# Second modulation and weight preparation on GpSimd, shared rotary keys projected ahead of the latent norm, three Newton steps

## The chip, the core and the metric

The kernel runs on one core of a Trainium2 chip. A core has five engines with a queue each: TensorE (PE in the profile; PEld is its loading of weights), VectorE (DVE), ScalarE (ACT), GpSimd (POOL) and SyncE (SP), which here only issues DMA transfers. An engine works through its queue in order; semaphores make it wait for others. The metric is the device time of one execution in microseconds, lower is better.

## The reference, cut to what matters

Two layers with adaptive layer norm over x of shape (8, 512, 128), that is 8 batches of 512 positions with 128 channels, everything in float32.

```python
def layer(x, c, wmod, attn, ffn):
    mod = (silu(c) @ wmod).reshape(8, 6, 1, -1)
    sa, ca, ga, sb, cb, gb = (mod[:, j] for j in range(6))
    ga = (2 * (ga >= 0) - 1) * maximum(abs(ga), 0.25)
    gb = (2 * (gb >= 0) - 1) * maximum(abs(gb), 0.25)
    x = x + ga * attn(layernorm(x) * (1 + ca) + sa)
    return x + gb * ffn(layernorm(x) * (1 + cb) + sb)
```

- Layer 0's attention is an RWKV time mix: each of the three projections of a mix of x and x shifted by one position, a recurrence over time with running maximum, then a projection. Its feed-forward is a linear layer with both operands quantized to a 6-bit grid in blocks of 32.
- Layer 1's attention has 16 heads of 32 plain and 64 rotary dimensions. A latent `x @ [w_cq, w_ckv]` is normed by its root mean square, 96 columns for the queries and 32 for keys and values. Three branches share the queries: causal attention on keys from the latent, with one rotary key `rope(x @ w_krope) / 16` shared by all heads; attention on the 32 positions of the highest score; and causal attention on keys straight from x. A softmax gate weighs the three.
- Layer 1's feed-forward is a gated recurrence over the 8 batches, each batch one step, whose final state enters every output.

## The kernel before, in words

**Layout.** Activations are held channels by positions, 128 x 512 a batch, or as four tiles of 128 positions by 128 channels for norms. Weights come in four packs (`pa` with layer 0's and the modulations, `pb` with layer 1's attention and a few of layer 0's, `pt` with the rotary tables, `pc` with the recurrence).

**Before the loop.** Up to the `manual_schedule` block the framework's scheduler orders every engine's queue: of the instructions that it takes to be ready, the one written first goes first. The source writes `modulate(0)`, the mixing weights, then the first `FIRST` = 14 steps of layer 0 for batch 0, then `remaining()`: the second modulation, the quantized weight of layer 0's linear layer, the scaling of the attention's weights by the norm's gains (L269 to L273), the halving of the recurrence's weights (L276), and the causal mask. After it the rest of layer 0 for batch 0, the preparation of batch 0, the first group's queries and keys, and the shared rotary keys follow, since the loop needs them.

**The loop.** Inside the block the order of PE, DVE, ACT and POOL is the order of the source. There are 192 units: 8 batches, 4 groups of 4 heads, 2 causal branches, and 3 parts of the triangle of positions. For each unit PE computes scores (`score`, L793), DVE adds the mask and reduces the rows (`lowered`, L805), ACT takes exponentials and sums (`raised`, L814), POOL divides (`normalised`, L823), PE transposes the result (`weigh`, L837; ACT copies it, L603), and PE multiplies with the values (`values`, L851). A unit's scores are written two units ahead of its transposition.

**Chains beside the loop.** Three generators run beside it: `layer0()` (mix and linear layer of each batch), `before()` (`prepare(b)`: norm, latent, shared keys, gate, the chosen 32 positions) and `recurrence()`. `advance` moves each by one step, four times a unit. A `yield 0` or `yield TR` goes on at the next advance, a smaller number waits for that many advances first, and `yield M` (M = 100) goes on only where `advance` is called with M, at the last of a unit's four. `need(name, b)` advances all chains until a step has been reached: `made` (the transposed latent nqT is there), `shared` (the rotary keys k1R are), `gate`, `chosen`.

**What the change touches.**
- `rsqrt` (L89 to L97): a first guess by integer arithmetic (L91) and four Newton steps of three DVE instructions each (L94, L95, L96), with a `yield 0` after each step. It is called in each layer norm (`ln_norm`: mix, linear, prepare, and two of the recurrence) and in the latent's norm.
- `modulate(l)` (L216 to L237): tanh on ACT, two DVE instructions, six matmuls, a copy out of PSUM (L228), and the rest on 128x8 pieces (L230 to L237), all on DVE.
- `prepare(b)` (L430 on): norm, transposition to hT (L442), the latent (L449, L451), its squares on POOL (L456), their sums (L460, L461), `rsqrt`, the scaling (L465 on DVE for the queries' 96 columns, L468 on POOL for the others), transposition (tpq) and copy to nqT (L475), a DMA of its last 32 rows to `latent` (L478), `made`; then `shared_keys`, `shared`; then the gate.
- `shared_keys(b)` calls `rotary`: two projections of hT (L638, named k1Rm), each multiplied twice by the tables on DVE (L619, L620, L624, L626), and a subtraction and an addition on POOL (L625, L627).
- The recurrence of a batch of layer 0 (L332 to L383): three scans on DVE, exponentials on ACT, a product (L364) and a sum (L372) on POOL, a division (L381, L383); then the output matmul (L386).

Of the kernel before, what the change touches and what calls it, by code (L numbers as in the profile page):

```python
# [14 lines left out]
ALU = mybir.AluOpType  # L15
# [3 lines left out]
B, T, D = 8, 512, 128  # L19
# [39 lines left out]
def adaln_kernel(ctx: ExitStack, tc: tile.TileContext, x, pa, pb, pc, pt, out):  # L59
# [29 lines left out]
    def rsqrt(dst, v, n, key):  # L89

        V.tensor_scalar(dst.bitcast(U32), v.bitcast(U32), -0.5, float(0x5F3759DF), ALU.mult, ALU.add)  # L91
        t = small.tile([128, n], FP, name=f"rt_{key}", tag=f"rt{n}")
        for _ in range(4):
            V.scalar_tensor_tensor(t, dst, -0.5, dst, ALU.mult, ALU.mult)  # L94
            V.tensor_tensor(t, t, v, ALU.mult)  # L95
            V.scalar_tensor_tensor(dst, t, 1.5, dst, ALU.add, ALU.mult)  # L96
            yield 0  # L97
# [117 lines left out]

    def modulate(l):  # L216
        c_in = WA[f"cT{l}"]

        sg = part(B)
        S.activation(sg, c_in, AF.Tanh, scale=0.5)  # L220
        si = sil0 if l == 0 else part(B)
        V.tensor_scalar(sg, sg, 0.5, 0.5, ALU.mult, ALU.add)
        V.tensor_tensor(si, sg, c_in, ALU.mult)
        ps = bank([128, 6, B], f"modps{l}")
        for j in range(6):
            PE.matmul(ps[:, j, :], lhsT=WA[f"wmod{l}"][:, j * 128 : (j + 1) * 128], rhs=si, start=True, stop=True)
        m = mods[l]
        V.tensor_copy(m, ps)  # L228
        for j in (1, 4):
            V.tensor_scalar(m[:, j, :], m[:, j, :], 1.0, None, ALU.add)  # L230
        for j in (2, 5):
            sgn = part(B)
            V.tensor_scalar(sgn, m[:, j, :], 0.0, 2.0, ALU.is_ge, ALU.mult)
            mag = part(B)
            V.scalar_tensor_tensor(mag, m[:, j, :], -1.0, m[:, j, :], ALU.mult, ALU.max)
            V.tensor_scalar(mag, mag, 0.25, None, ALU.max)
            V.scalar_tensor_tensor(m[:, j, :], sgn, -1.0, mag, ALU.add, ALU.mult)  # L237

    modulate(0)

# [10 lines left out]
    def remaining():  # L251

        modulate(1)


        wq = part(128, 4, 32)
        for _ in mx_quantize(
            wq, WA["fw"].rearrange("p (n k) -> p n k", k=32), 4,
            lambda n: part(128, 4, 32), "w",
        ):  # L260
            pass
        wps = bank([128, 128], "wps")
        PE.transpose(wps, wq.rearrange("p n k -> p (n k)"), ident)
        S.copy(wqT, wps)
        V.tensor_scalar(gbias, mod0[:, 5, :], WA["fbias"], None, ALU.mult)

        qscale = 1.0 / math.sqrt(HD)
        gq = part(1, rows=QL)
        V.tensor_scalar(gq, WB["g"][0:QL, :], qscale, None, ALU.mult)  # L269
        V.tensor_scalar(wd[0:QL, :], wd[0:QL, :], gq, None, ALU.mult)  # L270
        V.tensor_scalar(wd[QL:128, 0:512], wd[QL:128, 0:512], WB["g"][QL:128, :], None, ALU.mult)
        V.tensor_scalar(WB["wdk"][0:KVL, :], WB["wdk"][0:KVL, :], WB["g4"][0:KVL, :], None, ALU.mult)
        V.tensor_scalar(WB["wkr"], WB["wkr"], 1.0 / H, None, ALU.mult)  # L273

        for n in ("ufT", "uiT", "ucT", "uoT", "bf", "bi"):
            V.tensor_scalar(WC[n], WC[n], 0.5, None, ALU.mult)  # L276
# [153 lines left out]
    def prepare(b):  # L430
# [8 lines left out]
        transposed(tp, xn)  # L439
        hT = keep.tile([128, T], FP, name=f"hT1_{b}", tag="hT")  # L440
        hsum = small.tile([128, 1], FP, name=f"hsum_{b}", tag="hsum")
        S.activation(hT, tp, AF.Identity, bias=sa[:, b : b + 1], scale=ca[:, b : b + 1])  # L442
# [9 lines left out]
        sq = work("p2", [128, NC, 128], f"sq_{b}")  # L452
        yield 0
        hbc = pw.tile([128, 128], FP, name=f"hbc_{b}", tag="hbc")
        G.tensor_copy(hbc, hsum.to_broadcast([128, 128]))
        G.tensor_tensor(sq, cq, cq, ALU.mult)  # L456
        yield 1
        ss = small.tile([128, 2, NC], FP, name=f"ss_{b}", tag="ss")
        for i, (cols, n) in enumerate(((slice(0, QL), QL), (slice(QL, 128), KVL))):
            V.tensor_reduce(ss[:, i, :], sq[:, :, cols], AX.X, ALU.add)  # L460
            V.tensor_scalar(ss[:, i, :], ss[:, i, :], 1.0 / n, RMS_EPS, ALU.mult, ALU.add)  # L461
            yield 0
        rr = small.tile([128, 2, NC], FP, name=f"rr_{b}", tag="rr")
        yield from rsqrt(rr.rearrange("p k c -> p (k c)"), ss.rearrange("p k c -> p (k c)"), 2 * NC, f"rms{b}")
        V.tensor_tensor(  # L465
# [254 lines left out]
    def shared_keys(b):  # L720

        hT, nqT, _, _ = made_of[b]
        for i, _ in enumerate(rotary(pb_, "k1R", f"{b}", hT, WB["wkr"], (pw, ("p2", "p3")))):
# [147 lines left out]

    made_of, latent_of, k1_of, chosen_of, q_of, k3_of, v_of, sel_of, out_of, acc_of, pT_of, rot_of, xnf_of, h2_of = ({} for _ in range(14))

# [276 lines left out]
```

## Time and profile before

| | |
|---|---|
| time, median of 3 runs | 1703.07 us (1700.11 to 1705.38) |
| the profiled execution's span | 1703.6 us, 39936 instructions |
| granted TensorE clock, mean | 0.960 |
| first instruction of the loop's scores (L793) | 98.95 us |
| last projection of the attention (L862) | 1671.8 us |
| POOL's four forms of L823 | 426, 516, 620, 775 ns for 128, 256, 384, 512 columns |
| DVE multiplication 128x512 by a table (L624) | 676 ns |

How to read the profile's rows. A row of the time line has start and duration in us, engine, line, operation, what is written <- what is read, shape, and in brackets how long the engine was idle before it and whom it waited for. A row of the chain of waits has start, duration, engine, tile and line: it is followed back from the last instruction, each time to what released it. A row of the table by stage has the stretch, its length, the busy time (and count of instructions) of PE, PEld, DVE, ACT and POOL, the granted clock of TensorE as a fraction, the DMA share and GB/s. Matmul ends are modelled, so a busy PE is not a PE at its peak.

### The profile page before, as it was taken

How to read it: one execution, taken by the hardware profiler on the slowest of the kernel's cores; microseconds unless marked ns; L12 is line 12 of the kernel's file. 1: busy time of each engine (PE TensorE's matmuls, PEld its weight loads, DVE VectorE, ACT ScalarE, POOL GpSimd, SP SyncE). 2: the span in 40 equal slices, each digit the busy share in tenths (PEclk: the TensorE clock that was granted, in tenths of full speed). 3: DMA queues.
4: the chain of work that ended last, by engine and by line, in shares of the span. 5: the costliest groups of instructions: out<-in, count | busy, mean ns of one | idle time of the engine just before them, and what ended most of it. 6: DMA issues, size and time to landing. Idle time of an engine off the chain costs nothing.

```text
span 1703.6 us, 39936 instructions
## 1 busy us (share of the span) xinstructions
PE 1571.0 (92%) x14773; PEld 936.0 (55%) x14773; DVE 1267.4 (74%) x4262; ACT 1154.0 (68%) x3248; POOL 936.7 (55%) x1370
## 2 busy tenths in 40 slices
PE   3487999899999999999899999989999999999997
PEld 2244655555555655565456555655555665656663
DVE  6669868875789859876879769867789677756543
ACT  2144777665776867777666677766776777777883
POOL 2155567554666557564556457564566556655651
PEclk8578999998999999999999999999999999999999
DMA  4000000000000000000000000000000100000002
GB/s 170 0 3 1 2 1 4 7 2 13 3 2 8 8 8 4 1 8 14 3 2 2 8 8 3 2 2 20 3 2 14 32 14 3 2 14 14 1 11 66
DMA packets 13778, 20.55 MB, mean 12 GB/s; under 512 B 912, under 2 KB 9104, under 8 KB 13456
## 3 DMA queue, kind: packets, MB, share of 16 engines
q1 hardware_dynamic: 13584, 17.99, 3.1%
q8 instruction: 118, 1.93, 0.5%
q14 instruction: 76, 0.62, 0.1%
HBM read 11.70 MB, written 5.77 MB: 10 GB/s over the span
## 4 chain that ended last, share of the span: by engine, by line
PE 63%; DVE 26%; ACT 5%; issue 3%; POOL 3%; DMA 0%; POOLq 0%; SPq 0%; ACTq 0%; DVEq 0%
PE s L793 19%; PE t L837 12%; DVE p L805 7%; PE o L851 7%; PE s L755 2%; PE k3Rm L638 2%; PE qRm L638 2%; ACT p L814 2%; PE k3Np L610 1%; PE v1p L651 1%; PE op L862 1%; PE o L738 1%; PE qNp L610 1%; PE k0Np L610 1%; ACT pT L603 1%
## 5 line engine op out<-in xcount | busy, mean ns | idle before, releaser
L823 POOL TENSOR_SCALAR p<-p,rs 128x512 f32<-128x512 f32 (+3 forms) x1024 | 578.2, 584 | 389.3 <-DVE rs L819 219.1
L805 DVE CUSTOM_DVE_ANT_0 p<-s,mask 128x512 f32<-128x512 f32 (+3 forms) x1024 | 442.4, 477 | 177.5 <-PE s L793 175.5
L814 ACT ACTIVATE p<-p,nm 128x512 f32<-128x512 f32 (+3 forms) x1024 | 560.0, 553 | 14.1 <-DVE nm L805 13.9
L603 ACT COPY pT<-t 128x384 f32<-128x384 f32 (+1 forms) x768 | 354.6, 521 | 183.9 <-PE t L837 181.3
L837 PE MATMUL t<-ident,p 128*128 128x128 f32 x2560 | 367.2, 281 | 34.7 <-ACT pT L603 7.2
L837 PEld LDWEIGHTS t<-ident,p 128*128 128x128 f32 x2560 | 276.0, 142 | 160.1 <-issue 114.6
L814 ACT ACTIVATION_READ_ACCUMULATOR p<-p,nm 128x1 f32 x1024 | 196.8, 192 | 0.0
L793 PE MATMUL s<-k3R,qR 32*128 32x128 f32 (+3 forms) x2048 | 185.7, 453 | 4.4 <-DVE nm L805 3.2
L793 PE MATMUL s<-k1R,qR 32*128 32x512 f32 (+3 forms) x2048 | 186.2, 453 | 2.1 <-POOL k1R L625 2.1
L851 PE MATMUL o<-pT,v 128*32 128x512 f32 (+3 forms) x2048 | 153.2, 440 | 0.0
L793 PEld LDWEIGHTS s<-k3R,qR 32*128 32x128 f32 x2048 | 97.5, 186 | 83.4 <-DVE nm L805 30.8
L793 PEld LDWEIGHTS s<-k1R,qR 32*128 32x128 f32 x2048 | 105.7, 187 | 48.8 <-issue 15.2
L851 PEld LDWEIGHTS o<-pT,v 128*32 128x32 f32 x2048 | 60.4, 110 | 111.1 <-issue 100.3
L793 PE MATMUL s<-k0N,qN 32*128 32x512 f32 (+3 forms) x1024 | 102.4, 435 | 0.0
L793 PE MATMUL s<-k3N,qN 32*128 32x512 f32 (+3 forms) x1024 | 95.9, 431 | 0.0
L625 POOL TENSOR_TENSOR k3R<-k3R,rt_k3R 128x512 f32<-128x512 f32 x32 | 40.7, 1273 | 84.5 <-DVE rt_k3R L624 84.5
L805 DVE DVE_READ_ACCUMULATOR2_ANT nm<- 128x1 f32 x1024 | 82.4, 80 | 0.1
L765 POOL TENSOR_TENSOR p<-p,m 128x512 f32<-128x512 f32 x32 | 33.5, 1048 | 67.6 <-DVE m L764 67.6
L793 PEld LDWEIGHTS s<-k0N,qN 32*128 32x128 f32 x1024 | 60.4, 188 | 17.0 <-issue 2.5
L638 PE MATMUL qRm<-nqT,wb 96*128 96x512 f32 x128 | 68.6, 619 | 1.2 <-ACT nqT L475 0.7
L603 ACT COPY accT<-o 128x512 f32<-128x512 f32 x32 | 18.8, 586 | 71.1 <-PE o L851 71.1
L793 PEld LDWEIGHTS s<-k3N,qN 32*128 32x128 f32 x1024 | 54.4, 187 | 21.9 <-issue 14.9
(315 smaller groups left out, 2450.3 us busy)
## 6 DMA issues: line engine op xcount, KB each, us to landing
wb<-pb_dram SPq DMA_DIRECT2D x1, 3731.0 KB, 14.3
x<-x_dram SPq DMA_DIRECT2D x8, 256.0 KB, 4.1
x1all<-x SPq DMA_DIRECT2D x7, 256.0 KB, 2.0
h2all<-h SPq DMA_DIRECT2D x7, 256.0 KB, 2.0
h2o<-h2all SPq DMA_DIRECT2D x7, 256.0 KB, 2.6
x_first<-x1all SPq DMA_DIRECT2D x4, 256.0 KB, 3.4
out_dram<-x_first SPq DMA_DIRECT2D x4, 256.0 KB, 2.2
out_dram<-x SPq DMA_DIRECT2D x4, 256.0 KB, 2.3
```

The costliest lines, as they stand in the source:

```text
L603: S.copy(dst, src)
L610: PE.matmul(ps, lhsT=w[:, g * 128 : (g + 1) * 128], rhs=src, start=True, stop=True)
L625: G.tensor_tensor(lo, lo, r[0], ALU.subtract)
L638: PE.matmul(ps, lhsT=w[:, i * 128 : (i + 1) * 128], rhs=src, start=True, stop=True)
L755: PE.matmul(sp[h][to, :], lhsT=k[js, g, :], rhs=q[js, h * half : (h + 1) * half], start=(i == 0), stop=(i == 2), skip_group_check=True,)
L765: G.tensor_tensor(p2, p2, m2.unsqueeze(2).to_broadcast([128, T // 32, KEEP]), ALU.subtract)
L793: PE.matmul(un.s[j][:, at : at + n], lhsT=q[js, n - 128 : n], rhs=k[js, 0:n], start=(i == 0 and at == 0), stop=(i == 2), skip_group_check= ...
L805: V.tensor_tensor_reduce(out=un.p[:, j, at : at + n], in0=un.s[j][:, at : at + n], in1=mask[:, T - n :], scale=-1.0, scalar=3.4e38, op0=AL ...
L814: S.activation(p, p, AF.Exp, bias=un.nm[:, j, i : i + 1], scale=-1.0, accum_out=un.rs[:, j, i : i + 1])
L823: G.tensor_scalar(p, p, un.rs[:, j, i : i + 1], 1.0, ALU.mult, ALU.mult)
L837: PE.transpose(tp[:, k, :], un.p[:, j, at : at + 128], ident)
L851: PE.matmul(out_ps[js, c * 128 :], lhsT=v[:, c, js], rhs=pT[:, j, at[0] : at[-1] + 1 : step, :], start=not a and c == 0, stop=False, skip_ ...
```

## The change

Seven edits, in four places.

- `rsqrt`: three Newton steps in place of four, with one `yield 0` fewer.
- `modulate(l, E)`: the small arithmetic runs on the engine E: VectorE for layer 0, GpSimd for layer 1. The copy out of PSUM is ScalarE's for layer 1. The sign and the bound of 0.25 are formed with seven instructions of two inputs or fewer, in place of four.
- `remaining()` is called after 13 steps of layer 0 in place of 14 (the 13 hold one Newton step fewer, so it is the same place), and the scaling of attention and recurrence weights moves out of it into `attention_weights()`, on GpSimd, called after 11 further steps; the causal mask moves with it.
- `prepare`: the squares go ahead of `hbc` on GpSimd's queue; `shared_keys` moves from behind `made` to between the sums of squares and `rsqrt`, with a `yield M` ahead of it and a `yield 0` behind it; it takes hT from a table of its own.

```diff
-        for _ in range(4):
+        for _ in range(3):
             V.scalar_tensor_tensor(t, dst, -0.5, dst, ALU.mult, ALU.mult)
             V.tensor_tensor(t, t, v, ALU.mult)
             V.scalar_tensor_tensor(dst, t, 1.5, dst, ALU.add, ALU.mult)
             yield 0
...
-    def modulate(l):
+    def modulate(l, E):
...
-        V.tensor_scalar(sg, sg, 0.5, 0.5, ALU.mult, ALU.add)
-        V.tensor_tensor(si, sg, c_in, ALU.mult)
+        E.tensor_scalar(sg, sg, 0.5, 0.5, ALU.mult, ALU.add)
+        E.tensor_tensor(si, sg, c_in, ALU.mult)
...
-        V.tensor_copy(m, ps)
+        (S.copy if l else V.tensor_copy)(m, ps)
         for j in (1, 4):
-            V.tensor_scalar(m[:, j, :], m[:, j, :], 1.0, None, ALU.add)
+            E.tensor_scalar(m[:, j, :], m[:, j, :], 1.0, 0.0, ALU.add, ALU.add)
         for j in (2, 5):
-            sgn = part(B)
-            V.tensor_scalar(sgn, m[:, j, :], 0.0, 2.0, ALU.is_ge, ALU.mult)
-            mag = part(B)
-            V.scalar_tensor_tensor(mag, m[:, j, :], -1.0, m[:, j, :], ALU.mult, ALU.max)
-            V.tensor_scalar(mag, mag, 0.25, None, ALU.max)
-            V.scalar_tensor_tensor(m[:, j, :], sgn, -1.0, mag, ALU.add, ALU.mult)
-
-    modulate(0)
+            top, low, pos, neg = (part(B) for _ in range(4))
+            E.tensor_scalar(top, m[:, j, :], 0.25, 0.0, ALU.max, ALU.add)
+            E.tensor_scalar(low, m[:, j, :], -0.25, 0.0, ALU.min, ALU.add)
+            E.tensor_scalar(pos, m[:, j, :], 0.0, 1.0, ALU.is_ge, ALU.mult)
+            E.tensor_scalar(neg, pos, -1.0, 1.0, ALU.mult, ALU.add)
+            E.tensor_tensor(top, top, pos, ALU.mult)
+            E.tensor_tensor(low, low, neg, ALU.mult)
+            E.tensor_tensor(m[:, j, :], top, low, ALU.add)
+
+    modulate(0, V)
...
-        modulate(1)
-
+        modulate(1, G)
...
+    def attention_weights():
+
         qscale = 1.0 / math.sqrt(HD)
         gq = part(1, rows=QL)
-        V.tensor_scalar(gq, WB["g"][0:QL, :], qscale, None, ALU.mult)
-        V.tensor_scalar(wd[0:QL, :], wd[0:QL, :], gq, None, ALU.mult)
...
+        G.tensor_scalar(gq, WB["g"][0:QL, :], qscale, 0.0, ALU.mult, ALU.add)
+        G.tensor_scalar(wd[0:QL, :], wd[0:QL, :], gq, 1.0, ALU.mult, ALU.mult)
...
         for n in ("ufT", "uiT", "ucT", "uoT", "bf", "bi"):
-            V.tensor_scalar(WC[n], WC[n], 0.5, None, ALU.mult)
+            G.tensor_scalar(WC[n], WC[n], 0.5, 1.0, ALU.mult, ALU.mult)
...
+        G.tensor_tensor(sq, cq, cq, ALU.mult)
         hbc = pw.tile([128, 128], FP, name=f"hbc_{b}", tag="hbc")
         G.tensor_copy(hbc, hsum.to_broadcast([128, 128]))
-        G.tensor_tensor(sq, cq, cq, ALU.mult)
...
         rr = small.tile([128, 2, NC], FP, name=f"rr_{b}", tag="rr")
+        yield M
+        yield from shared_keys(b)
+        ready.add(("shared", b))
+        yield 0
         yield from rsqrt(rr.rearrange("p k c -> p (k c)"), ss.rearrange("p k c -> p (k c)"), 2 * NC, f"rms{b}")
...
         ready.add(("made", b))
-        yield M
-        yield from shared_keys(b)
-        ready.add(("shared", b))
         yield M
...
-    FIRST = 14
+    FIRST, SECOND = 13, 11
...
     remaining()
+    for _ in range(SECOND):
+        next(stages[0])
+    attention_weights()
```

More of the change, by code (lines that the diff above doesn't have):

```diff
@@ L265, in remaining @@
         V.tensor_scalar(gbias, mod0[:, 5, :], WA["fbias"], None, ALU.mult)
+    def attention_weights():
         qscale = 1.0 / math.sqrt(HD)
         gq = part(1, rows=QL)
-        V.tensor_scalar(gq, WB["g"][0:QL, :], qscale, None, ALU.mult)
[L270 to L273, printed above, removed]
+        G.tensor_scalar(gq, WB["g"][0:QL, :], qscale, 0.0, ALU.mult, ALU.add)
+        G.tensor_scalar(wd[0:QL, :], wd[0:QL, :], gq, 1.0, ALU.mult, ALU.mult)
+        G.tensor_scalar(wd[QL:128, 0:512], wd[QL:128, 0:512], WB["g"][QL:128, :], 1.0, ALU.mult, ALU.mult)
+        G.tensor_scalar(WB["wdk"][0:KVL, :], WB["wdk"][0:KVL, :], WB["g4"][0:KVL, :], 1.0, ALU.mult, ALU.mult)
+        G.tensor_scalar(WB["wkr"], WB["wkr"], 1.0 / H, 1.0, ALU.mult, ALU.mult)
         for n in ("ufT", "uiT", "ucT", "uoT", "bf", "bi"):
-            V.tensor_scalar(WC[n], WC[n], 0.5, None, ALU.mult)
+            G.tensor_scalar(WC[n], WC[n], 0.5, 1.0, ALU.mult, ALU.mult)
         G.memset(mask, 0.0)
@@ L440, in prepare @@
         hT = keep.tile([128, T], FP, name=f"hT1_{b}", tag="hT")
+        hT_of[b] = hT
         hsum = small.tile([128, 1], FP, name=f"hsum_{b}", tag="hsum")
@@ L720, in shared_keys @@
     def shared_keys(b):
-        hT, nqT, _, _ = made_of[b]
+        hT = hT_of[b]
         for i, _ in enumerate(rotary(pb_, "k1R", f"{b}", hT, WB["wkr"], (pw, ("p2", "p3")))):
@@ L869, in project @@
             nc.sync.dma_start(out=x1_all[b], in_=xs[b])
-    made_of, latent_of, k1_of, chosen_of, q_of, k3_of, v_of, sel_of, out_of, acc_of, pT_of, rot_of, xnf_of, h2_of = ({} for _ in range(14))
+    made_of, latent_of, k1_of, chosen_of, q_of, k3_of, v_of, sel_of, out_of, acc_of, pT_of, rot_of, xnf_of, h2_of, hT_of = ({} for _ in range(15))
     class Unit:
```

## The prediction

> **What bounds the kernel now.** I read the page's busy times and chain first, then busy time by stage.
>
> ```profile
> PE 1571.0 (92%) x14773; PEld 936.0 (55%) x14773; DVE 1267.4 (74%) x4262; ACT 1154.0 (68%) x3248; POOL 936.7 (55%) x1370
> ...
> PE 63%; DVE 26%; ACT 5%; issue 3%; POOL 3%; DMA 0%; POOLq 0%; SPq 0%; ACTq 0%; DVEq 0%
> ```
>
> ```profile
> 0.00:40.00 40.00, 13.69 (x42) 8.42 (x43) 28.18 (x105) 7.93 (x15) 9.98 (x17) 0.83 0.48 181
> 40.00:66.00 26.00, 7.52 (x18) 3.18 (x16) 13.38 (x41) 2.42 (x4) 4.62 (x5) 0.50 0.00 0
> 66.00:99.00 33.00, 22.60 (x48) 9.81 (x48) 19.51 (x82) 8.04 (x13) 7.41 (x8) 0.60 0.01 3
> ...
> 160.00:1660.00 1500.00, 1441.39 (x14109) 868.94 (x14103) 1139.75 (x3832) 1090.30 (x3103) 874.89 (x1291) 0.98 0.02 7
> 1660.00:1704.00 44.00, 34.74 (x151) 15.95 (x149) 14.79 (x42) 16.23 (x31) 7.75 (x12) 0.94 0.23 71
> ```
>
> After the stretch and its length these rows give PE, PEld, DVE, ACT and POOL busy, then the granted clock. There are two kernels here. From 160 to 1660 us PE is busy 96% and little can be won. The first 99 us are one serial chain for batch 0: PE is busy 44 of 99 us, and most of the chain goes through DVE. Microseconds taken out of that chain move everything behind them. So I look at the DVE and POOL rows of the time line before the first output matmul (L386, 39.20 us), the last serial stretch, and what POOL did.
>
> ```profile
> 25.02 0.18 DVE L228 COPY mod<-modps 128x48 f32<-128x48 f32 x1
> 25.14 1.22 DVE L368 TENSOR_TENSOR_SCAN bb<-d,d 128x512 f32<-128x512 f32 x1
> 26.28 1.24 DVE L230 TENSOR_SCALAR mod<-mod 128x8 f32<-128x8 f32 x2
> ...
> 28.81 1.02 DVE L270 TENSOR_SCALAR wb<-wb,start 96x1536 f32<-96x1536 f32 x1
> ...
> 30.94 0.67 DVE L371 TENSOR_TENSOR e<-bb,e 128x512 f32<-128x512 f32 x1
> ...
> 31.88 0.74 DVE L276 TENSOR_SCALAR wc<-wc 128x128 f32<-128x128 f32 x6
> ...
> 33.25 1.64 DVE L377 SCALAR_TENSOR_TENSOR e<-er,e 128x512 f32<-128x512 f32 x1
> ```
>
> ```profile
> 25.27 2.14 POOL L364 TENSOR_TENSOR aa<-aa,e 128x512 f32<-128x512 f32 x1 [2.35 <-DVE mod L228]
> 31.16 3.18 POOL L372 TENSOR_TENSOR v<-v,aa 128x512 f32<-128x512 f32 x1 [3.74 <-DVE v L363]
> ```
>
> The second modulation (to 28.13) and the attention weights (28.13 to 30.34, and L276) sit in DVE's queue in front of the recurrence of batch 0. Then the last pieces of the chain before the loop:
>
> ```profile
> 86.69 2.72 PE qRm L638 x4
> 89.41 1.71 PE qNp L610 x2
> 91.12 2.00 PE k0Np L610 x2
> 93.12 3.73 PE k1Rm L638 x4
> 96.87 0.70 DVE rt_k1R L624
> 97.64 1.27 POOL k1R L625
> 98.95 1.21 PE s L793
> ```
>
> The first scores wait for the shared keys, which are projected last.
>
> **The change, part by part** (against the profiled span of 1703.6 us; the median of the runs, 1703.07, is 0.03% under it, so I add nothing around the span).
>
> A. *DVE relieved before 39 us.* L228 goes to ACT, which is idle there from 26.2 to 41.3. Of the DVE rows, 0.12 (L228), 26.28 to 30.34 = 4.06, and 31.88 to 32.55 = 0.67 go: 4.85 us. But L371 overwrites what POOL's L364 reads, and that ended at 27.41; L371 then starts at 27.41 instead of 30.94, so 3.53 + 0.67 = 4.2 us can be won, 5.2 if L377's 0.97 us of waiting (1.64 against 0.67) goes too. Against that, 16 GpSimd instructions of 128x8 (2 + 2x7) now stand ahead of L364 in the source's order. The trace has none of that size; the nearest rows are a 128x1 memset at 0.10 and a 128x128 copy at 0.29, so 1.6 to 4.6 us. With L364 ready at 25.0 but DVE's scan and L363 filling 25.1 to 27.0, the worst case is L364 from 31.6 to 32.7 against 27.4: +5.3, net +1.1. If the scheduler lets L364 through first the price is about 0. I take 0.2 us each and some two thirds of them ahead, a delay of 2.2: **-2.0**, ends -5.2 and +1.1. The weights, by the L823 rows (128x128 426 ns, 128x512 775 ns, so 0.31 + 0.00091 per element), are 1.7 + 2x0.78 + 0.54 + 4x0.43 + 3x0.31 = 6.4 us of POOL. They come after the 11 further steps, so behind L372, and POOL was idle from 34.34 to 49.85: costed at nothing; without that cover L408 would be late, then the first quantization.
>
> A rule speaks against this part. The Trainium skill, "SBUF — State Buffer", section "SBUF: two separate sides", says that GpSimd and a DVE instruction with two SBUF inputs, or in a two-port mode, exclude each other for a whole instruction. The rows look like that: L377 ends 0.55 us after L372 ends. By the page, a running 96x1536 weight could hold up L383 by 1.7 us, and the total below would be -13.5 (an estimate from the L823 rows); by the row it stays inside A's bounds.
>
> B. *First modulation and first norm.* 14 small DVE instructions in place of 8, start to start 0.075 us: +0.45. The dropped Newton step (L94 11.28, L95 12.07, L96 12.29) was woven in between: three slots, -0.25; xn was queued behind and could now run in DVE's idle 8.99 to 11.15, at best -1.9. I take **-0.2**, ends +0.5 and -1.9.
>
> C. *Newton, first linear norm*: the fourth step ran alone from 47.26 to 47.86: **-0.6**. D. *Newton, first attention norm*: 69.50 to 70.09: **-0.5** (0 to -0.6).
>
> E. *Latent norm to nqT* (nqT at 86.05). The fourth step went from 82.04 to 84.37, stuck behind the scan of batch 1 and POOL's L335; gone, rr is ready at 79.4. But four DVE multiplies (4x0.68) and two POOL adds (2x1.27) of the shared keys now stand ahead of it, and on PE 2x1.7 us of matmul at half clock ahead of batch 1's six, which had ended at 84.1 with the transposition tpq at 85.36. PE then ends these near 85 to 87. **-1.0**, ends +1.5 and -4.0.
>
> F. *Shared keys out of the last stretch.* After k0Np (ends 93.12) the scores can start, since qR was finished by POOL at 92.70: 98.95 - 93.12 = **-5.8**, ends -6 and -2 (if POOL's adds for qR slip).
>
> G. *Newton in the loop.* 34 calls x 3 instructions; all L94 to L96 groups sum to 102.4 us, so 25.6 us of DVE work goes, some 23 of it past 99 us. DVE is on the chain for 26% of the span and busy for 74%: 0.35 of each DVE microsecond counts, 8 us; half of that I give to the next wait in line (PE). **-4.5**, ends 0 and -9.
>
> H. *Tail.* Batch 7's norm is bare: its last step runs from 1678.00 to 1678.59: **-0.6**.
>
> *Other moves, costed at nothing.* Counted from the yields and the four advances of each unit, nqT comes about two units later than before in batches 2 to 7, still two to seven units ahead of its query projection, and for batch 1 it stays in unit 17 with the projection at the end of 19. The DMA to latent goes with it on SP's queue, which holds nothing urgent. If that slack were gone, PE would wait for transposition, copy and that 2.0 us DMA. The sq multiplication ahead of hbc on POOL gains 0.3 us of an uncritical row.
>
> Sum: -2.0 - 0.2 - 0.6 - 0.5 - 1.0 - 5.8 - 4.5 - 0.6 = -15.2, so 1703.6 - 15.2 = **1688 us**.
>
> **Rivals.**
> 1. *The loop doesn't feel DVE.* PE is busy 96% from 160 to 1660 us; G is 0. For it: PE's own share of the chain, 63%. Against: DVE small instructions stand on it too. 1703.6 - 10.7 = **1693**.
> 2. *The early reordering doesn't take.* Before the loop the framework's scheduler, not the source, orders the queues, and the moved work may land elsewhere: POOL's small instructions all ahead of L364 (+1.1), tpq behind everything (+1.5), F only -2. Then +1.1 - 0.2 - 0.6 - 0.5 + 1.5 - 2.0 - 4.5 - 0.6 = -5.8: **1698**.
> 3. *Slower: the rotation falls into the wrong unit.* In each of batches 1 to 7 the shared keys' four DVE multiplies (2.7 us) now stand three units earlier, beside the latent norm's reductions, ahead of the row reductions L805 for which ACT waits. If all is exposed: 7 x 2.7 = 18.9, and G is eaten: 1703.6 - 10.7 + 18.9 = **1712**. It decides from (10.7 + 5.1)/7 = 2.3 us a batch. Against it: the same multiplies stood before in units just as full.
>
> **How the numbers follow.** Forecast 0.65 (its ends in A, B, E and G, partly cancelling, 1681 to 1696); rival 1 0.17; rival 2 0.08; rival 3 0.10. 0.3% (5.1 us, about what these runs can tell from no change) lies at 1698.0 and 1708.2. Faster holds the forecast, rival 1 and a little of rival 2: 0.85. Same: 0.07, from rival 2 and a weak rival 3. Slower: 0.08. The range reaches past rival 1 to rival 2 above and to both gains' far ends below: 1677 to 1698.
>
> **What would show it.** A right: L386 starts by 37.5, no 96x1536 row on DVE; wrong: POOL L364 starts after 29. E: nqT between 82 and 87.5. F right: k1Rm ahead of qRm and the first L793 near 88 to 90; wrong if it still starts after 95. G: total of L94 to L96 near 77 us and the time from the first L793 to the end (1604.6 now) shorter by about 5; unchanged is rival 1; longer by over 11 is rival 3. The prediction is wrong if that last stretch moves by more than 9 us either way.

## The result, and the profile after

| | before | after |
|---|---|---|
| time, median (range) | 1704.22 us (1700.11 to 1705.53, 4 runs) | 1719.95 us (1717.17 to 1725.57, 4 runs) |
| ratio, after to before | | 1.0102, interval 1.0078 to 1.0125 |
| profiled execution: time / span | 1705.38 / 1703.6 us | 1717.17 / 1715.4 us |
| first L805 (after: L810) row reduction, unit 0 | 104.47 us | 96.69 us |
| the same, unit 6 | 162.14 us | 157.27 us |
| the same, unit 190 of 192 | 1649.54 us | 1661.91 us |

The change makes the kernel slower by 1.0%; the forecast was 0.9% faster. The profiled executions differ by 11.8 us, and the last three rows say where. Up to the loop's first row reduction the changed kernel is 7.8 us ahead. The first six units give back 2.9. From unit 6 to unit 190 it loses 17.2 (1504.6 us against 1487.4). The tail wins 0.6. Not all of the 7.8 is the change's. Kernels 7 and 8 below run before's instructions up to there, and their first reduction comes at 99.93 and 101.48 us, where TensorE's granted clock from 66 to 99 us is 0.71, with 0.60 in before and 0.75 in after. Against them the changed kernel is only 3.2 and 4.8 us ahead. Of the 2.9 some 2.2 are not the change's either: kernels 7 and 8 take 59.9 and 59.8 us from unit 0 to unit 6, before 57.7, after 60.6. (Unit n means here, in the profile, the stretch from the first row reduction of unit n to that of unit n + 1. Reductions are written two units ahead, so in this stretch runs what iteration n - 2 of the loop's source writes.)

Busy times and chain of the page of after:

```profile
PE 1576.3 (92%) x14773; PEld 940.1 (55%) x14773; DVE 1250.1 (73%) x4142; ACT 1154.7 (67%) x3249; POOL 948.1 (55%) x1399
...
PE 67%; DVE 22%; ACT 5%; POOL 4%; issue 2%; DMA 0%; POOLq 0%; ACTq 0%; DVEq 0%
```

DVE is indeed relieved, by 17.3 us (1267.4 to 1250.1), its share of the chain falls from 26 to 22%, and the span grows all the same. The table by stage of after (stretch, length, then PE, PEld, DVE, ACT, POOL busy with counts, granted clock, DMA share, GB/s):

```profile
0.00:40.00 40.00, 15.52 (x43) 8.71 (x43) 23.70 (x84) 8.07 (x16) 18.74 (x46) 0.85 0.48 181
...
66.00:99.00 33.00, 24.58 (x80) 11.97 (x80) 21.16 (x70) 10.32 (x19) 8.54 (x8) 0.75 0.01 3
...
160.00:1660.00 1500.00, 1431.38 (x13943) 859.36 (x13945) 1116.96 (x3709) 1076.14 (x3057) 864.15 (x1270) 0.98 0.02 7
```

In the same 1500 us of the loop PE now does 1431.4 us of work instead of 1441.4, and DVE 1117.0 instead of 1139.8: both have more idle time, so neither engine's total sets the pace. The loop lost because work met in the wrong units, which kernels 14 and 15 below show.

**Before 40 us.** The rows of POOL, then of DVE, then of PE:

```profile
25.57 1.10 POOL L233 TENSOR_SCALAR start<-mod 128x8 f32<-128x8 f32 x1
26.64 0.25 POOL L234 TENSOR_SCALAR start<-mod 128x8 f32<-128x8 f32 x1
...
27.08 0.26 POOL L233 TENSOR_SCALAR start<-mod 128x8 f32<-128x8 f32 x1
...
29.04 1.26 POOL L367 TENSOR_TENSOR aa<-aa,e 128x512 f32<-128x512 f32 x1
...
31.17 1.54 POOL L274 TENSOR_SCALAR wb<-wb 32x512 f32<-32x512 f32 x1
32.81 1.86 POOL L273 TENSOR_SCALAR wb<-wb,start 96x1536 f32<-96x1536 f32 x1
...
36.04 0.68 POOL L275 TENSOR_SCALAR wb<-wb 32x512 f32<-32x512 f32 x1
```

```profile
25.37 1.25 DVE L371 TENSOR_TENSOR_SCAN bb<-d,d 128x512 f32<-128x512 f32 x1
...
30.34 0.69 DVE L374 TENSOR_TENSOR e<-bb,e 128x512 f32<-128x512 f32 x1 [3.71 <-POOL aa L367]
...
31.55 0.68 DVE L377 TENSOR_TENSOR e<-e,q 128x512 f32<-128x512 f32 x1
```

```profile
38.32 2.05 PE L389 MATMUL o<-v,wb 128*128 128x512 f32 x2 [13.44 <-issue]
```

All sixteen small instructions stand ahead of the recurrence's product (L364 before, L367 here), which runs from 29.04 to 30.30 where it ended at 27.41. DVE idles 3.71 us for it. What the emptier DVE won goes into this wait, and the output matmul starts 0.9 us earlier (39.20 to 38.32). Kernel 2 below, which has the shorter Newton iteration and nothing of the GpSimd part, starts it at 37.75.

**From the latent's norm to the scores.** The chain of waits (start, duration, engine, tile, line):

```profile
80.90 0.67 DVE d L340
81.57 0.92 DVE rt_rms L95
82.49 0.60 DVE q L343
...
83.29 0.69 DVE ev L349
...
85.76 1.13 PE tpq L126 x4
86.89 0.02 issue
86.91 0.59 ACT nqT L483
...
92.87 1.05 PE k0Np L615 x2
93.92 2.79 PE s L798 x24
```

The root is still woven into batch 1's recurrence (d, q, ev), one Newton step shorter or not, and nqT comes at 86.91 (before 86.05), 17.2 us after hT in place of 14.3. But nothing stands any more between k0Np and the scores: the first score row is at 93.46 where it was at 98.95.

**In the loop, unit 52.** This is the largest single loss; in after the unit lasts 15.5 us, before 6.2. First the table by stage around it in after, then in before:

```profile
523.80:536.60 12.80, 12.51 (x106) 7.61 (x105) 9.49 (x24) 7.16 (x19) 3.56 (x5) 1.00 0.06 22
536.60:552.10 15.50, 7.25 (x79) 2.87 (x81) 12.53 (x38) 4.09 (x17) 10.21 (x10) 0.67 0.00 1
```

```profile
533.10:545.10 12.00, 11.11 (x90) 6.97 (x90) 11.78 (x28) 6.80 (x18) 7.01 (x8) 1.00 0.01 1
545.10:551.30 6.20, 6.08 (x82) 2.66 (x84) 5.90 (x24) 4.57 (x18) 4.76 (x6) 1.00 0.13 46
```

PE works 7.25 of 15.5 us. The time lines of PE and POOL in after say what it waits for:

```profile
543.50 1.08 PE L760 MATMUL s<-qR,sR 32*32 32x256 f32 x8 [5.78 <-POOL sR L630]
547.05 1.50 PE L760 MATMUL s<-qR,sR 32*32 32x256 f32 x20 [2.47 <-DVE sV L722]
```

```profile
538.01 3.80 POOL L828 TENSOR_SCALAR p<-p,rs 128x512 f32<-128x512 f32 x4 [1.52 <-DVE rs L824]
541.77 1.26 POOL L162 TENSOR_TENSOR q<-q,m 128x512 f32<-128x512 f32 x1
542.99 0.45 POOL L630 TENSOR_TENSOR sR<-sR,rt_sk 128x128 f32<-128x128 f32 x1
```

L760 is the scores of the third branch, on the 32 chosen positions. It stands in PE's fixed order, and its keys sR are only being made: their last sum L630 is queued on POOL behind the loop's division (L828) and a step of the quantization (L162). PE waits 5.78 us for it and then 2.47 us until DVE has written the chosen values (sV). In before the same sum (L627 there) ended at 540.46 and the values (L717) at 542.65, ahead of the unit's start at 545.1:

```profile
539.15 0.90 POOL L625 TENSOR_TENSOR sR<-sR,rt_sk 128x128 f32<-128x128 f32 x1
540.01 0.45 POOL L627 TENSOR_TENSOR sR<-sR,rt_sk 128x128 f32<-128x128 f32 x1
```

### The profile page after: what moved, and what is told of

Same layout as the page of the kernel before. It is cut to its first block, busy times and chain, and to the rows that moved or that the text cites. A ratio compares the mean times of both kernels' runs of the same rounds, so it can differ in the third digit from the quotient of the medians.

```text
span 1715.4 us, 39852 instructions
## 1 busy us (share of the span) xinstructions
PE 1576.3 (92%) x14773; PEld 940.1 (55%) x14773; DVE 1250.1 (73%) x4142; ACT 1154.7 (67%) x3249; POOL 948.1 (55%) x1399
## 4 chain that ended last, share of the span: by engine, by line
PE 67%; DVE 22%; ACT 5%; POOL 4%; issue 2%; DMA 0%; POOLq 0%; ACTq 0%; DVEq 0%
PE s L798 21%; PE t L842 13%; PE o L856 7%; DVE p L810 6%; PE s L760 2%; POOL p L828 2%; PE qRm L643 2%; PE k3Rm L643 2%; ACT p L819 2%; PE v1p L656 1%; PE o L743 1%; PE k3Np L615 1%; PE op L867 1%; PE qNp L615 1%; PE v0p L656 1%
## 5 line engine op out<-in xcount | busy, mean ns | idle before, releaser
L828 POOL TENSOR_SCALAR p<-p,rs 128x512 f32<-128x512 f32 (+3 forms) x1024 | 580.1, 589 | 413.7 <-DVE rs L824 238.0
L810 DVE CUSTOM_DVE_ANT_0 p<-s,mask 128x512 f32<-128x512 f32 (+3 forms) x1024 | 442.5, 477 | 197.4 <-PE s L798 196.9
L842 PE MATMUL t<-ident,p 128*128 128x128 f32 x2560 | 362.9, 280 | 31.8 <-DVE k3R L625 7.0
L798 PE MATMUL s<-k3R,qR 32*128 32x512 f32 (+3 forms) x2048 | 189.5, 457 | 4.5 <-DVE nm L810 3.6
L798 PE MATMUL s<-k1R,qR 32*128 32x512 f32 (+3 forms) x2048 | 189.8, 457 | 2.4 <-DVE nm L810 2.4
L798 PEld LDWEIGHTS s<-k1R,qR 32*128 32x128 f32 x2048 | 106.7, 188 | 50.6 <-issue 17.2
L630 POOL TENSOR_TENSOR k3R<-k3R,rt_k3R 128x512 f32<-128x512 f32 x32 | 40.7, 1273 | 80.1 <-DVE rt_k3R L629 80.1
L810 DVE DVE_READ_ACCUMULATOR2_ANT nm<- 128x1 f32 x1024 | 82.6, 81 | 0.0
L798 PEld LDWEIGHTS s<-k3N,qN 32*128 32x128 f32 x1024 | 56.1, 187 | 21.6 <-issue 14.5
```

The lines of the kernel that those rows point to most:

```text
L630: G.tensor_tensor(lo, lo, r[0], ALU.subtract)
L798: PE.matmul(un.s[j][:, at : at + n], lhsT=q[js, n - 128 : n], rhs=k[js, 0:n], start=(i == 0 and at == 0), stop=(i == 2), skip_group_check= ...
L810: V.tensor_tensor_reduce(out=un.p[:, j, at : at + n], in0=un.s[j][:, at : at + n], in1=mask[:, T - n :], scale=-1.0, scalar=3.4e38, op0=AL ...
L828: G.tensor_scalar(p, p, un.rs[:, j, i : i + 1], 1.0, ALU.mult, ALU.mult)
L842: PE.transpose(tp[:, k, :], un.p[:, j, at : at + 128], ident)
```

## The experiments

Each kernel is one edit of the kernel before or of the changed one. The stretch from unit 6 to unit 190 of the profiled execution is given beside the median, as "loop"; it is 1487.4 us before and 1504.6 after, and is free of what happens in the opening. It comes from one execution, and kernels with the same order of instructions differ in it by some 4 us (see 11 to 13), so where loop and ratio disagree, the ratio counts. A ratio compares a median with that of the kernel before, timed alongside. The diffs are cut to what matters; not all lines that leave an old place are shown.

The theories at the start. **Y**: the fourth step's `yield` is a slot, a place in the loop's order that work can take; with one fewer, the chains beside the loop move against the units. **K**: the shared keys ahead of the root put DVE work of batches 1 to 7 into the wrong units. **P**: the GpSimd part costs.

**1. newton_only.** Three steps; nothing else.

```diff
-        for _ in range(4):
+        for _ in range(3):
...
-    FIRST = 14
+    FIRST = 13
```

> The kernel before with three Newton steps in place of four, and nothing else (13 first steps, so the same place for what follows). Theory K (the loss of about 16 us is the moved shared keys, whose two M gates now stand ahead of nqT): the step's chain savings count and nothing else moves: 1694 to 1699 us. Theory Y (the loss comes of the removed yields: the chains beside the loop run out of step with the units they were laid beside): 1712 us or more. Theory P (the instructions moved to GpSimd cost the loop something): 1694 to 1699.

Measured: 1711.64 us against 1701.52, ratio 1.0055 (1.004 to 1.007); loop 1498.3. Fewer instructions, and slower. Unit 52 lasts 16.2 us.

**2. newton_keep_yield.** The same three steps, with the fourth step's slot left empty.

```diff
-        for _ in range(4):
+        for _ in range(3):
...
             V.scalar_tensor_tensor(dst, t, 1.5, dst, ALU.add, ALU.mult)
             yield 0
+        yield 0
```

> The kernel before with three Newton steps, but with the fourth step's yield kept, so that every chain beside the loop has the same steps in the same slots as before and only DVE instructions are missing. Theory K: 1694 to 1699 us. Theory Y: also 1694 to 1699, and faster than the kernel with three steps and no yield by 13 us or more. A time of 1703 would say that the Newton steps in the loop are hidden by PE and that only some 2 us of the opening and the tail count.

Measured: 1691.05 us, ratio 0.9942 (0.9922 to 0.9962); loop 1477.8, unit 52 lasts 6.2 us. The two kernels issue the same instructions; one empty `yield` is worth 20.6 us.

**3. newton_caught_up.** As 1, but batch 1's chains are brought up as far as they were before, by three more advances at the end of iteration 26.

```diff
+        if i == 26:
+            need("chosen", 1)
+            for _ in range(3):
+                advance(M)
```

> Three Newton steps without the fourth yield, and three extra advances of all chains at unit 26, where the kernel before needed four forced advances for the chosen keys of batch 1 and the kernel with fewer yields needs one. Counted from the yields, the chains then stand from batch 2 on where they stood before, and the chosen keys of batch 2 are ready at unit 50's first slot, not forced at its end. Theory Y, made sharper (the loss of 20 us is this late catching up, with the forced stretch at unit 50): 1690 to 1697 us, and no unit of 16 us at unit 52. If the loss comes of the shorter gaps inside a batch: still above 1705.

Measured: 1704.84 us against 1703.6, ratio 1.0007 (0.9993 to 1.0021); loop 1493.8, unit 52 back at 6.2 us. The late catch-up is real, but it is only 4.5 us of the 20.5 between the loops of kernels 1 and 2, or by the ratios 8 of 19. What is left are the slots that still move, within batches and before unit 26: the loop of kernel 3 loses there in pieces of one to three microseconds, and what makes each of them is not shown.

**4. yield_gone_in_root.** As 2, but the slot is dropped in the latent's root alone (the root calls `rsqrt` with a key of its own).

```diff
+        if not key.startswith("rms"):
+            yield 0
```

> Three Newton steps; the fourth step's yield is kept in every layer norm and dropped only in the latent's root, so root and nqT of each batch stand one slot earlier and no other chain moves. Theory Y in its narrow form (only the late catch-up and the moved chains cost): 1688 to 1694, as with all yields kept. Wide form (any slot that moves costs): 1695 or more.

Measured: 1689.2 us against 1704.85, ratio 0.9909 (0.9885 to 0.9932); loop 1478.6. Dropping this slot costs nothing. What costs is dropping it in the layer norms, which moves whole chains against the loop.

**5. keys_only.** The shared keys ahead of the root, four steps, no GpSimd part.

```diff
         rr = small.tile([128, 2, NC], FP, name=f"rr_{b}", tag="rr")
+        yield M
+        yield from shared_keys(b)
+        ready.add(("shared", b))
+        yield 0
...
         ready.add(("made", b))
         yield M
-        yield from shared_keys(b)
-        ready.add(("shared", b))
-        yield M
```

> The kernel before with the shared rotary keys projected ahead of the latent's root, and nothing else. Theory K: the opening gains about 6 us and the loop loses 18 to 22: 1716 to 1720 us. Theory Y or P: the opening's gain alone, 1696 to 1699 us.

Measured: 1725.21 us against 1701.52, ratio 1.0134 (1.0116 to 1.0153); loop 1504.0. At unit 0 it is 5.4 us ahead of before, but only 0.8 and 2.4 ahead of kernels 7 and 8, whose clock there is like its own (0.72 and 0.71). From unit 6 on it loses in steps, the larger of them at units 18 to 20, 40, 63 to 65 and 131 to 134, where each batch's root, scaling and nqT now come (two units later than before).

**6. keys_after_root.** The same keys between the root and the scaling, so that the root keeps its old unit.

```diff
         yield from rsqrt(rr.rearrange(...
+        yield M
+        yield from shared_keys(b)
+        ready.add(("shared", b))
+        yield 0
         V.tensor_tensor(
             cq[:, :, 0:QL], ...
```

> The kernel before with the shared keys between the latent's root and the scaling of the latent, where the changed kernel has them ahead of the root. The root's 13 small DVE instructions keep their old slots; keys come one unit later than with keys ahead of the root; scaling, transposition and nqT come as late as there. Theory R (the loss of keys_only is the root, pushed two units back into the units where DVE and GpSimd have the recurrence of the next batch): most of the 24 us is won back, 1699 to 1708 us. Theory L (the loss is the late scaling and nqT, or the keys' own rotation in a full unit): 1718 us or more.

Measured: 1715.63 us against 1703.6, ratio 1.0074 (1.0054 to 1.0094); loop 1502.9, only 1.1 us less than in 5. The ratios say more: 1.0074 against 1.0134, with intervals apart, so the root's place is worth up to 0.6% (10 us; the keys, too, come a unit later here). Something over 0.7% is left for scaling and nqT two units late and for the early keys. The next two kernels separate the keys from the rest: with the keys in a chain of their own, one can move while the other stays.

**7. keys_alone_early.** Batches 1 to 7: keys two units early, everything else in its old unit.

```diff
+    def keys_alone(b, wait):
+        for _ in range(wait):
+            yield M
+        yield from shared_keys(b)
+        ready.add(("shared", b))
...
         rr = small.tile([128, 2, NC], FP, name=f"rr_{b}", tag="rr")
+        if b:
+            chains[keys_alone(b, 0)] = M
```

> For batches 1 to 7 the shared keys alone run two units earlier (as in the changed kernel), as a chain of their own; root, scaling, transposition and nqT stay in their old units; four Newton steps, batch 0 as before. Theory E (the early rotation itself crowds a unit): 1712 to 1722, with the batch periods of the kernel with the keys moved. Theory L (what costs is the latent's scaling, transposition and nqT two units late): within 0.3% of before, 1698 to 1708.

Measured: 1713.44 us against 1704.85, ratio 1.0055 (1.004 to 1.007); loop 1500.9. Between the two theories: the early rotation does cost. For batch 3 it is nearly even: units 64 and 65, which the rotation leaves, get 0.1 and 1.2 us shorter (9.7 to 9.6, 6.7 to 5.5), and units 62 and 63, which it enters, 0.3 and 1.2 longer (10.0 to 10.3, 5.9 to 7.1). The largest loss is batch 5's: unit 109 lasts 11.5 us in place of 5.8, and in it PE stands idle for 5.76 us ahead of the scores of the chosen positions; the profile puts that wait down to the last multiplication of the early rotation. It is a stall like that of unit 52.

**8. scaling_alone_late.** The counterpart: keys in their old units, root, scaling, transposition and nqT two units late.

```diff
+        if b:
+            chains[keys_alone(b, 2)] = M
+            yield M
+            yield M
+            yield 0
         yield from rsqrt(rr.rearrange(...
```

> The counterpart: the shared keys stay in their old units, and root, scaling, transposition and nqT of batches 1 to 7 come two units later, as in the kernel with the keys moved. Theory L: 1712 to 1722, with steps at units 18 to 20, 40 to 42, 63 to 65 and so on. Theory E: within 0.3% of before. If both kernels lose about half, the two costs add up; if neither loses, it is the combination that costs.

Measured: 1724.51 us, ratio 1.0113 (1.0096 to 1.013); loop 1506.4. Both moves cost, the late root and scaling more: 19.7 us of the median against 8.6, and 19.0 us of the loop against 13.5. Whether they add up stays open: together (kernel 5) they cost 23.7 us of the median, not far from the sum of 28.3, but only 16.6 of the loop, where the sum is 32.5. Neither theory holds alone. Unit 64, where batch 3's root now stands, shows the mechanism. By stage in this kernel, units 62 to 64:

```profile
632.00:641.70 9.70, 9.70 (x85) 5.45 (x78) 6.37 (x17) 7.38 (x18) 7.24 (x11) 1.00 0.00 0
641.70:648.30 6.60, 6.00 (x71) 4.42 (x71) 6.50 (x19) 6.38 (x16) 2.70 (x4) 1.00 0.01 2
648.30:662.50 14.20, 12.58 (x86) 6.38 (x88) 13.99 (x38) 8.98 (x30) 8.77 (x9) 0.88 0.01 2
```

and in before, the same units:

```profile
628.40:638.40 10.00, 10.00 (x89) 6.18 (x81) 9.72 (x27) 7.96 (x19) 8.20 (x12) 1.00 0.00 0
638.40:644.30 5.90, 5.67 (x64) 4.04 (x63) 5.90 (x16) 5.87 (x14) 2.69 (x4) 1.00 0.01 4
644.30:654.00 9.70, 8.37 (x72) 3.92 (x71) 9.70 (x28) 7.16 (x25) 8.15 (x8) 1.00 0.03 8
```

Before, root and scaling stood in unit 62, where PE is busy 10.00 of 10.00 us. Taking them out relieves DVE by 3.35 us (9.72 to 6.37) and shortens the unit by 0.3, since PE is still full. In unit 64 DVE was already busy 9.70 of 9.70 us, with the recurrence's scans and two rotations. There the same work adds itself whole: DVE 4.29 us more, the unit 4.5 longer. The added rows, on DVE in this kernel:

```profile
652.09 0.58 DVE L94 SCALAR_TENSOR_TENSOR rt_rms<-rr 128x8 f32<-128x8 f32 x1
652.71 0.63 DVE L95 TENSOR_TENSOR rt_rms<-rt_rms,ss 128x8 f32<-128x8 f32 x1
...
654.06 1.23 DVE L94 SCALAR_TENSOR_TENSOR rt_rms<-rr 128x8 f32<-128x8 f32 x1
...
660.92 1.63 DVE L471 TENSOR_TENSOR cq<-cq,rr 128x384 f32<-128x384 f32 x1
662.47 0.55 DVE L818 CUSTOM_DVE_ANT_0 p<-s,mask 128x384 f32<-128x384 f32 x1
```

The scaling L471 stands directly ahead of the row reductions (L818), and followed back from these the chain of waits runs through DVE alone for the whole unit. A Newton instruction on 128x8 (usually 0.17 us) lasts up to 1.23 between the scans.

**9. keys_first_batch.** On kernel 2, the keys ahead of the root for batch 0 alone, where the chain is serial.

```diff
         rr = small.tile([128, 2, NC], FP, name=f"rr_{b}", tag="rr")
+        if b == 0:
+            yield M
+            yield from shared_keys(b)
+            ready.add(("shared", b))
+            yield 0
...
-        yield from shared_keys(b)
-        ready.add(("shared", b))
-        yield M
+        if b:
+            yield from shared_keys(b)
+            ready.add(("shared", b))
+            yield M
```

> Three Newton steps with the fourth yield kept, and the keys ahead of the root for batch 0 alone, so that the loop is that of newton_keep_yield (1691 us) and only the opening differs. If the opening's gain stays: 1685 to 1688 us. If the first units give it back (in keys_only the first row reduction came 5.4 us earlier, but unit 6 only 0.6): 1690 to 1692.

Measured: 1690.21 us against 1703.6, ratio 0.992 (0.9902 to 0.9937); loop 1478.7. The interval overlaps that of kernel 2 (0.9942), and the 1.5 us that unit 0 is earlier than there in the profiles is 0.1 at unit 6.

**10. keys_early_kept.** Kernel 9 with the keys of batches 1 to 7 early too, as in 7.

```diff
+        else:
+            chains[keys_alone(b, 0)] = M
```

> Three Newton steps with all slots kept, shared keys of all batches early but in a chain of their own, so that root, scaling and nqT stay in their old units; batch 0 with the keys ahead of the root. Theory L: 1686 to 1694, as with the keys of batch 0 alone moved. Theory E: 1700 to 1712.

Measured: 1691.55 us against 1704.85, ratio 0.9924 (0.9904 to 0.9944); loop 1482.7, 4.0 us more than in 9. With a DVE that has one Newton step less to do, the early keys cost 4 us of the loop instead of 13.5, and nothing that the medians can tell.

**11. pool_only, 12. modulate_only_pool, 13. weights_only_pool.** The GpSimd part alone, then its halves, with four steps and the keys in their old place.

```diff
-        modulate(1)
+        modulate(1, G)
...
-    FIRST = 14
+    FIRST, SECOND = 14, 11
...
+    for _ in range(SECOND):
+        next(stages[0])
+    attention_weights()
```

Kernel 12 keeps the first of these edits (with the new `modulate`), kernel 13 the others (the new `modulate` too, but on VectorE).

> The kernel before with the second modulation and the weights on GpSimd (and the seven instructions for sign and bound), four Newton steps and the keys at their old place. All of it is over before the loop. Theories K and Y: 1701 to 1704 us (the first output matmul moved from 39.20 to 38.32 in the changed kernel). Theory P: slower by 5 us or more, seen in the loop.

> Second modulation on GpSimd alone; weights on DVE in their old place, four Newton steps, keys as before. Theory: the weights cost, so this is 1702 to 1705, or faster. Rival: the sixteen small instructions ahead of the recurrence's product cost, so this shows the slowdown of the whole GpSimd part, 1707 or more.

> Weight preparation on GpSimd, after eleven more steps of layer 0, alone; second modulation on DVE in its old place. Theory: the weights cost, 1707 or more. Rival: 1702 to 1705.

Measured: 1707.94 us against 1701.52, ratio 1.0036 (1.0024 to 1.0047), for the whole part; 1709.04 against 1703.91, ratio 1.0027 (1.0013 to 1.0042), for the modulation; 1702.92, ratio 0.9995 (0.9978 to 1.0011), for the weights. So the cost, about 5 us, is the modulation's move to GpSimd and not the weights, opposite to the theory that I wrote down. In the loop these three have before's order of instructions (but for the squares of the latent, which stand ahead of hbc on GpSimd), and it takes 1487.8, 1484.3, 1492.4 and, in before, 1487.4 us: a profile of one execution tells a loop to within some 4 us. The loss is in the opening, as far as the rows show it. The output matmul starts at 42.70 us in kernel 11, at 41.26 in kernel 12 and at 38.90 in kernel 13, against 39.20 in before, and nqT comes 3.5 and 2.1 us late in kernels 11 and 12 (89.57 and 88.12 against 86.05). In both the recurrence's product waits for all sixteen small instructions (it starts at 31.26 and 31.57, in before at 25.27), and the recurrence's first scan is late already (20.78 and 20.32 against 19.52). What the medians lose beyond these 3.5 and 2.1 us stays open.

**14. after_keep_yield, 15. after_old_slots.** The changed kernel with the slot of the fourth step kept; then also with the keys of batches 1 to 7 back in their old units, as a chain of their own, and root, scaling and nqT where they were.

```diff
+        yield 0
...
+        if b == 0:
+            yield M
+            yield from shared_keys(b)
+            ready.add(("shared", b))
+            yield 0
+        else:
+            chains[keys_alone(b, 2)] = M
```

> The changed kernel with the fourth step's yield kept, nothing else: the chains stand where keys_only has them, with fewer DVE instructions. From keys_only (1725 us) less the 10 us that the missing instructions brought, plus 2 to 6 us of pool_only: 1716 to 1721 us. If the lost yields were the cause of the changed kernel's time, it would be 1700 or less.

> All seven edits of the change, but every chain keeps its old slots in the loop: the fourth step's yield is kept, and for batches 1 to 7 the shared keys stay in their old units, as a chain of their own, with root, scaling and nqT where they were. Batch 0 as in the changed kernel. If the slots are the whole cause: 1688 to 1699 (the time with three steps and kept yields, up to some 6 us worse for the GpSimd part). If the GpSimd part or something else carries a large share of the loss: 1702 or more.

Measured: 1707.18 us against 1703.6, ratio 1.0036 (1.0019 to 1.0054), loop 1494.2; then 1695.54 against 1703.91, ratio 0.995 (0.9932 to 0.9968), loop 1479.9. All seven edits are in the last kernel, with the arithmetic of the changed one; only the slots differ, and it is 0.5% faster than before where the changed kernel is 1.0% slower. The slots of the loop are the cause of the loss. The fastest kernels of the study are 4, 9, 2 and 10 (1689.2 to 1691.55 us), which the runs can't tell apart.

## Why the prediction was wrong

**The step that failed** is "Other moves, costed at nothing". I had counted from the yields that nqT comes two units later and asked only whether its reader still has it in time. It has: in the loop of after no instruction of PE waits for nqT. What I left out is what the moved instructions displace in the unit that they land in, and I counted nqT alone:

- *The yield.* I had booked the lost slot under G as DVE work saved. Counted again for every chain: before, the chosen keys of batch 1 are fetched at the end of iteration 26 with four forced advances of all chains; with one slot fewer it takes one, and from batch 2 on every chain stands about a unit later (layer 0 of batch 2 ends in iteration 31 instead of 30). The chosen keys of batch 2 then have to be forced at the end of iteration 50, instead of being ready at its start, and in the stretch of unit 52, which is that iteration, PE waits for them. Price by kernels 1 and 2: 20.6 us, of which the late chosen keys are some 8 (kernel 3).
- *The keys.* Their move costs 23.7 us with four steps (kernel 5) and 11.6 in the changed kernel (1707.18 against 1695.54, kernels 14 and 15).

The two are not simply added: 1719.95 to 1707.18 to 1695.54 is 12.8 and 11.6 us, 24.4 together. The forecast was -15.2 us and +15.7 was measured; 24.4 of these 31 are the slots. The rest, some 7, is that the edits without their slots give -8.4 (kernel 15) and not -15.2.

**Rival 3** ("the rotation falls into the wrong unit", 1712, chance 0.10) had the mechanism and was nearest, with the wrong instruction in front: the rotation's four multiplications cost less than the root and scaling that they push back (kernels 7 and 8), and counted again they stand one unit earlier in batches 2 to 7 of the changed kernel, not three. Its sign was a stretch from the first score row to the end that is longer by over 11 us; it is longer by 17.3 (1604.6 to 1621.9). Its argument against itself, "the same multiplies stood before in units just as full", is what kernel 8's table by stage answers: units 62 and 64 are about as full, but what leaves a unit in which another engine is full too gives next to nothing back, and what enters a unit in which DVE is full costs all of it. This is shown for batch 3's root and scaling; for most other steps of the loop the displaced work is not shown. Rival 1 falls: the loop does feel DVE (kernel 2). Rival 2 came true in the opening for A and E, not for F.

Point by point, by the signs that the prediction named:

- **A**, -2.0: wrong, and not only in size. The output matmul is 0.9 us early, but kernel 2, without any of A, has it earlier still (37.75 against 38.32), and A alone makes it late (kernels 11 and 12). The sign for "wrong" (product after 29) holds with 29.04. I let a third of the small instructions' time pass behind the product; all of it came ahead. An extra 0.84 us looks like contention: the first L233 lasted 1.10 and ended 0.05 after DVE's scan L371, its twin with no scan beside it 0.26. The weight L274 lasted 1.54 while DVE ran L366 and L377, its twin L275 of the same shape 0.68. That is what the Trainium skill, "SBUF — State Buffer", section "SBUF: two separate sides", says of GpSimd against a DVE instruction with two SBUF inputs; the rows agree. But the hold-up that I priced by the page on DVE (1.7 us) did not come in after: the product that I had named (L383, there L386) started at 37.53, after the 96x1536 weight was done, and took 0.69; L377 lasted its usual 0.68 beside L274, and it was GpSimd that waited. In kernel 11 a hold-up of that kind did come: L366 lasted 1.95 us, in place of 0.69 in after, beside the 96x1536 weight L273, and ended 0.53 us after it. Cover for the weights held, kernel 13.
- **B**, -0.2: +0.2 at the recurrence's first scan (19.52 to 19.74), inside its ends; the dropped step alone gives -0.4 there (19.12 in kernel 2).
- **C, D**, -1.1: right. From the output matmul to hT 32.6 us became 31.4.
- **E**, -1.0: wrong, and beyond its end of +1.5. From hT to nqT 14.3 us became 17.2, and 17.8 in kernel 5, where the keys alone move; kernel 2, with the keys in their old place, has 14.5. The keys' rotation stands ahead of the root, and the root is stuck in batch 1's recurrence as before. So nqT is 0.9 us late, where A to E should have brought it to 81.8.
- **F**, -5.8: right in kind. The 5.8 us from the end of k0Np to the first score row are gone. But the term's size is the clock's: that stretch is 4.4 us in kernels 2, 7, 8, 11 and 12, whose order there is before's and whose four key projections take 2.0 us in place of 3.8. From nqT to the first score row 12.9 us became 6.55, and 8.9 is what kernels 7, 11 and 12 take for it in the old order. Unit 0's row reduction is 7.8 us earlier, or 3.2 to 4.8 against kernels 7 and 8, and A to F said 10.1.
- **G**, -4.5: right in kind, too small. The instructions L94 to L96 go from 102.4 to 78.3 us (77 named). With all slots kept the loop is shorter by 9.6 us, that is 0.43 of the 22.3 us of DVE work gone from it (1139.8 from 160 to 1660 us, 1117.5 from 160 to 1644 in kernel 2). My 0.35 was near; the half that I then gave "to the next wait in line" was wrong. Against -6.2 for C, D, G and H, kernel 2 gained 10.5 in all.
- **H**, -0.6: 0.6 in these two profiles, which proves little: the same tail takes 52.4 to 56.1 us in the kernels with four steps.
- *Around the span* I added nothing; 1.8 us lie there in both profiled executions (1705.38 - 1703.6).

## What to carry to other kernels

In a loop whose engine queues are written out by hand, a `yield` is a time slot: removing work and removing its slot are two edits, so keep the slot first, measure, and move slots only afterwards. When work moves to another unit, look up which engine is full in the unit that it leaves and in the unit that it enters; that a reader still has slack says nothing about either. Count every chain's slots, forced advances too, not only those of the tile that the diff moves.

## What the runs showed of the hardware

The granted TensorE clock makes the opening differ between executions with the same instructions. Kernels 1 and 3 have the same instructions in the same order up to the loop's iteration 26; by stage, first kernel 1, then kernel 3:

```profile
66.00:99.00 33.00, 25.22 (x60) 11.19 (x64) 16.21 (x54) 7.84 (x13) 8.01 (x8) 0.60 0.01 3
```

```profile
66.00:99.00 33.00, 23.84 (x74) 10.85 (x74) 17.72 (x58) 8.67 (x16) 8.85 (x8) 0.79 0.01 3
```

With a clock of 0.60 the first row reduction comes at 101.7 us, with 0.79 at 97.4. So 4.3 us in the opening are no effect of an edit, and a step of 1 us there can't be read from one profile; before's own opening, at 0.60, is one of the slow ones. The Trainium skill, "TensorE: Matmul & The Clock Gate", section "Part 1: The HAM clock gate", says that this ramp varies from run to run and is less than 1% of a span; the rows agree (4.3 of 1712 is 0.25%), though in a comparison of a fraction of a per cent it is as large as the thing measured. A stall also costs after it has ended: in the 15.5 us of unit 52 in after, with PE idle for half of them, the granted clock is 0.67, where before it is 1.00 through the same unit. From 548 to 550 us PE works again, 2.00 of 2.00 us, and the clock is still 0.51; from 550 us on it is 1.00.
